# Query and key projections in seven block products instead of eight, on one core

## The chip, the cores and the metric

The kernel runs on one core of a Trainium2 chip. The metric is the device time of one execution in microseconds; less is better. Engines are named as in the profile: PE is TensorE (its matmuls; PEld its weight loads), DVE is VectorE, ACT is ScalarE, POOL is GpSimd, and SP is SyncE, which here only issues transfers. All numbers are fp32.

## The reference

The input is `x` of shape (8, 512, 32, 32): eight batch elements, 512 channels, 1024 positions. Two layers follow each other. Layer 0 is a group norm, a projection to queries, keys and values, attention in 8 heads of 64 channels, an output projection, a second group norm and a residual. Layer 1 is single-headed attention over 512 channels with normalized weights.

```python
# layer 0
hn = group_norm(x, gn1_scale, gn1_bias)
qkv = jnp.einsum('bchw,oc->bohw', hn, w_qkv) + b_qkv[None, :, None, None]
qkv = qkv.reshape(b * NHEAD, 3 * ch, n)
q, k, v = jnp.split(qkv, 3, axis=1)
scale = ch ** (-0.25)
wgt = jnp.einsum('bct,bcs->bts', q * scale, k * scale)
wgt = jax.nn.softmax(wgt, axis=-1)
a = jnp.einsum('bts,bcs->bct', wgt, v).reshape(b, c, h, w)
out = jnp.einsum('bchw,oc->bohw', a, w_proj) + b_proj[None, :, None, None]
out = group_norm(out, gn2_scale, gn2_bias)
return x + out
# layer 1: qkv = w_qkv x, divided by its rms; softmax(q k / sqrt(512)) v; w_out; (x + h) / sqrt(2)
```

The change concerns the lines that make `q` and `k` in layer 0.

## The kernel before

Every operation is issued through a wrapper that keeps the program's order on each engine, so the order in the text is the order in which each engine works. (All instructions carry the line of that wrapper, L34, in the profile; they are told apart by tile names.)

*Loops.* The outer loop runs over the eight elements `b`. For each, layer 0's attention runs in 32 steps `i`. The heads are taken in four pairs `j`, 8 steps to a pair; a step handles 128 query positions of both heads. Then come the end of layer 0 (`finish_layer0`), layer 1 (`Layer1.project`, which also holds the score stage with its four weight units, tiles `e`), and layer 1's products (tiles `po` with `e`), the last three of which are spread as fills over the next element's steps 0 to 2.

*A step* (`Heads.step`): the row maxima of both heads on DVE (`nm<-s`) and exponentials on ACT (`p<-s,nm`); then, on every second step from 5 on, the products with v of an earlier pair of steps (`po<-pT,v`); then the step's fill, usually one piece of a projection (`pqk`); then the scores of the next step (`s`); the transpose of the p of the step before on DVE (`pb<-p`), and four transfers on SP that rearrange it (`pT<-pb`); last, the reciprocal of the row sums on DVE and the scaling of p by it on POOL (`p<-p,tt`). What is in `later` follows the scaling; the adds of a projection (`due`) are there. On elements 1 to 6, POOL also normalizes a fourth of the next element's input in steps 1, 3, 5 and 7 (`hn<-hn,a,c`).

*Buffers.* Score tiles rotate through three PSUM buffers of two banks each, two tiles a step; so the second tile of step i+1 needs the buffer that the first exponential of step i frees. Projection pieces and value products rotate through two single banks. `pb` and the `p` tag have two buffers each.

*The projection of a pair* (`project_rows`), spread over the 8 steps of the pair before: for k, then q, and each half of the positions, one piece of 4 × 2 matmuls of 64 rows, which work side by side in the two halves of the array. The upper rows of channels give one PSUM bank, the lower rows the other; ACT evicts both (into `qk`, and into `v#`, the spare end of the `v` tile), and POOL adds them. That is 4 pieces, 8 block products (2 outputs, 2 halves of positions, 2 halves of rows), 32 matmuls a pair. A matmul of the program is two PE instructions in the profile. Pieces run in steps 0, 3, 4, 6 of pair 0's steps for elements from 1 on, and otherwise in steps 0, 2, 4, 6 of each pair's eight.

*Weights.* Three places in SBUF are shared in time: `qk` (the q and k weights, then layer 0's output operands, then layer 1's score operands), `v` (the v weights, then layer 1's value operands) and `p` (the Gram matrix of layer 1, which stays until the last element needs the plain output weights). `fetch` brings them back from DRAM copies through SP. `qk` and `v` are fetched in the score stage for the next element.

*Setup.* Weights are transposed on PE (`turn`), operands of seven-product schemes for the other projections are formed, and copies of all are stored to DRAM.

Of the kernel before, what the change touches and what calls it, by code (L numbers as in the profile page):

```python
# [8 lines left out]
F32 = mybir.dt.float32  # L9
I32 = mybir.dt.int32  # L10
AF = mybir.ActivationFunctionType
# [41 lines left out]
def attention_blocks_kernel(  # L53
# [52 lines left out]
    def big(name, lead=CI):  # L106

        return slots.take([P, lead, CI * N // lead], name)
# [14 lines left out]
    def run(pieces):  # L123
        for _ in pieces:
            pass
# [61 lines left out]
    cols = const.tile([P, NCOLS], F32, name="cols")  # L187
    bqs = const.tile([P, CI], F32, name="bqs")
    bpd = const.tile([P, 2], F32, name="bpd")

    def col(base, i):
        return cols[:, base + i : base + i + 1]
# [13 lines left out]
    def rsqrt(r, v, n, name):  # L206
# [3 lines left out]

    CH = C // 2
    places = {
        "qk": ("qk", [P, 2, CI, C]), "score": ("qk", [P, 7, 2, CH]),
        "v": ("v", [P, 7, 2, CH]), "value": ("v", [P, 7, 2, CH]),
        "proj": ("p", [P, CI, C]), "gram": ("p", [P, CI, C]), "proj7": ("qk", [P, 7, 2, CH]),
    }
    far = {
        name: dram.tile([P, CI, C] if name == "v" else shape, F32, tag=f"far_{name}", name=f"far_{name}")
        for name, (_, shape) in places.items()
    }  # L220
    near = {}
    far_rinv = dram.tile([NT, P], F32, tag="far_rinv", name="far_rinv")

    def place(name, b):
        tag, shape = places[name]
        near[name] = weights.tile(shape, F32, tag=f"w_{tag}", name=f"{name}_{b}")
        if name == "v":

            flat = near[name].rearrange("p k h c -> p (k h c)")
            near["v#"] = flat[:, CI * C :]  # L230
            near[name] = flat[:, : CI * C].rearrange("p (ci c) -> p ci c", ci=CI)
        return near[name]

    def fetch(name, b):
        SY.dma_start(out=place(name, b), in_=far[name])

    def turn(wrows, dst, k):

        for half in range(2):
            pt = ps_s.tile([P, 2, CI, P], F32, tag="sc", name=f"wT_{k}_{half}")  # L240
            for jj in range(2):
                for ci in range(CI):
                    PE.transpose(pt[:, jj, ci, :], wrows[:, 2 * half + jj, ci * P : (ci + 1) * P], ident)
            o = dst[:, :, 2 * half * P : 2 * (half + 1) * P].rearrange("p ci (jj o) -> p jj ci o", jj=2)
            for jj in range(2):
                if jj:
                    AC.copy(o[:, jj], pt[:, jj])
                else:
                    VE.tensor_copy(o[:, jj], pt[:, jj])


    def gn_stats(st, src, k):
# [85 lines left out]
    def project_qk(b, j, hn):  # L338

        qk = pair.tile([P, 2, N], F32, tag="qk", name=f"qk_{b}_{j}")  # L340
        kp = qk[:, 1, :].rearrange("p (be m) -> p be m", be=4)

        def pieces():
            for t in (1, 0):
                w = near["qk"][:, t]
                for th in range(2):
                    hs = slice(th * HN, (th + 1) * HN)
                    pm = bank(f"pqk_{b}_{j}_{t}_{th}")
                    run(matmuls(pm, [(w[:, ci, j * P : (j + 1) * P], hn[:, ci, hs]) for ci in range(CI)]))
                    if t == 0:  # L350
                        AC.activation(qk[:, 0, hs], pm, AF.Identity, bias=bqs[:, j : j + 1], scale=QSCALE0)
                    else:
                        AC.activation(
                            kp[:, :, th * P : (th + 1) * P],
                            pm.rearrange("p (m be) -> p be m", be=4),
                            AF.Identity,
                            bias=col(BK, j),
                        )
                    yield

        return qk, pieces()

    def project_rows(b, j, hn):

        qk = pair.tile([P, 2, N], F32, tag="qk", name=f"qk_{b}_{j}")
        kp = qk[:, 1, :].rearrange("p (be m) -> p be m", be=4)
        spare = near["v#"]

        def pieces():
            for t in (1, 0):
                w = near["qk"][:, t]
                scale = 1.0 if t else QSCALE0
                bias = col(BK, j) if t else bqs[:, j : j + 1]
                for th in range(2):
                    hs = slice(th * HN, (th + 1) * HN)
                    pms = [bank(f"pqk_{b}_{j}_{t}_{th}_{r}") for r in range(2)]
                    for ci in range(CI):
                        for r in range(2):  # L380
                            PE.matmul(
                                pms[r],
                                w[halves[r], ci, j * P : (j + 1) * P],
                                hn[halves[r], ci, hs],
                                start=(ci == 0),
                                stop=(ci == CI - 1),
                            )
                    to, rest = qk[:, 0, hs], spare[:, hs]
                    if t:

                        to = kp[:, :, th * P : (th + 1) * P]
                        rest = rest.rearrange("p (be m) -> p be m", be=4)
                        pms = [pm.rearrange("p (m be) -> p be m", be=4) for pm in pms]
                    AC.activation(to, pms[0], AF.Identity, bias=bias, scale=scale)
                    AC.activation(rest, pms[1], AF.Copy, scale=scale)
                    yield lambda to=to, rest=rest: PO.tensor_add(to, to, rest)

        return qk, pieces()

# [324 lines left out]
    class Layer1:  # L724
# [7 lines left out]
            self.right = self.rhs.columns  # L732
            self.e, self.sums = {}, {}

        def project(self):
            b, xt = self.b, self.xt
            v = self.v = big(f"v1_{b}", NT)
            xy = prob.tile([P, 2, N], F32, tag="p", name=f"xy_{b}")
# [1 line left out]
            for cj in range(CI):  # L740
# [5 lines left out]
                VE.tensor_mul(part if cj else acc, py.rearrange("p a f -> p (a f)"), xt[:, cj, :])  # L746
                if cj:
                    VE.tensor_add(acc, acc, part)
            if b + 1 == B - 1:
                fetch("proj", b + 1)  # L750

            ss = ps_m.tile([P, NT, 2], F32, tag="mm", name=f"ss_{b}")
            rinv = self.rinv = small.tile([P, NT], F32, tag="rinv", name=f"rinv_{b}")
# [105 lines left out]
                        square_sums()  # L859
                        broadcast()  # L860
            if b + 1 < B:
                fetch("qk", b + 1)
            sums = sum_u()
            for m in range(4):
                for k, _ in enumerate(value_unit(m).steps()):
                    if (m, k) in ((2, 0), (2, 4), (3, 1), (3, 5)):
                        next(sums, None)
            if b + 1 < B:
                fetch("v", b + 1)
            for m in range(4):  # L870
                run(weight_unit(m).steps())
            Seven.drain()
            Seven.half = None
            slots.give(f"u_{b}")
# [31 lines left out]
    gram = place("gram", 0)  # L906

    def turn_w0(t, name):
        near_t, far_t = (near["v"], far["v"]) if t == 2 else (near["qk"][:, t], far["qk"][:, t])
        turn(w0rows[t], near_t, name)  # L910
        SY.dma_start(out=far_t, in_=near_t)

    def operands(name, w, s7):

# [46 lines left out]
    SY.dma_start(out=far["gram"], in_=gram)  # L961
    VE.tensor_copy(cols[:, :GQKV], pcol)
    VE.tensor_scalar_mul(bqs, cols[:, BQ : BQ + CI], QSCALE0)
    VE.tensor_sub(bpd, cols[:, BP + 2 : BP + 4], cols[:, BP : BP + 2])
    next(coeffs)

# [24 lines left out]
    for name in ("w1_qk", "w1_vo"):  # L991
        slots.give(name)
    turn_w0(1, "k")
    v0_0 = big("v0_0", NT)
    v0 = project_v0(0, x0, v0_0)
    for _ in range(NT // 2):
        next(v0)
    turn_w0(0, "q")
    operands("value", value, [prob.tile([P, 4, 2, CH], F32, tag="p", name=f"value7_{i}") for i in range(2)])
    turn(wprow, proj, "p")  # L1000
    qk0, todo = project_qk(0, 0, x0)
# [2 lines left out]
    d3 = done3.rearrange("p (k h) c -> p k (h c)", k=2).rearrange("p k (i h c) -> p k i h c", h=2, c=CH)  # L1004
    operands("proj7", proj, [d3[:, k] for k in range(2)])
    SY.dma_start(out=far["proj"], in_=proj)
    for name in ("rows_kq", "rows_vp", "done1", "done2", "done3"):
        slots.give(name)


# [3 lines left out]
    heads.scores(0)  # L1014
    for b in range(B):
        hn, more = heads.hn, b + 1 < B
        todo = iter(())
        for i in range(STEPS):
            j, r = divmod(i, NB)
            due = []  # L1020

            projects = (i - LAG) % RG if not b or i not in (2, 3) else i == 3
            fill = [lambda: due.append(next(todo, None))] if projects else []
            early, later = [], []
            if i < CI:
                fill, later = fills[i] + fill, laters[i]
            if r == 0:
                if j + 1 < CI:
                    heads.qk[j + 1], todo = project_rows(b, j + 1, hn)
                elif more:  # L1030
                    qk_next, todo = project_rows(b + 1, 0, hn_next)
                if j + 1 == CI:
                    slots.give(f"hn_{b}")
                    if not more:
                        o_last = big(f"o_{b}")
                        todo = project_out_half(b, heads, o_last)
            later.append(lambda: [f() for f in due if f])

            if b and more and i % 2 and i < 2 * CI:
                later.append(lambda: norm1.apply(i // 2, PO))  # L1040
            if not b:
# [15 lines left out]
                if 0 <= k - 7 < CI // 2:  # L1057
                    for ci in range(2):
                        later.append(lambda ci=ci: norm1.apply(2 * (k - 7) + ci, PO))

            if i == STEPS - NB + 1:
                xt = big(f"x_{b}")
# [26 lines left out]
            finish_last(b, heads, xt, o_last, begun)  # L1089
        fetch("value", b)  # L1090
        one = Layer1(b, xt)
        one.project()
        hn_now, steps = hn_next, iter(())

        def norm_step():
# [75 lines left out]
```

## Time and profile before

| | us |
|---|---|
| median of 3 runs | 3283.85 (3283.36 to 3284.07) |
| the profiled execution | 3283.51 |
| its span, first to last instruction | 3281.5 |
| mean granted PE clock | 0.998 |
| one element, e.g. start of layer 1 (`py`) of element 1 to that of element 2 | 1136.99 − 739.74 = 397.25 |
| of it, the 32 attention steps (element 1, 494.22 to 679.92) | 185.7 |

The page gives busy time by engine; then the chain of work that ended last, as shares; then groups of instructions with their number, busy time, mean duration and the idle time before them. A row of the timeline has the start, the length, the engine, the operation with its tiles and shapes, how many instructions are merged, and in brackets the idle time before it with what ended it. Busy times of overlapping instructions are counted once, so a group's busy time is the time its engine gave to it.

### The profile page before, as it was taken

To read this page: it belongs to the slowest core of one execution; us is meant where nothing else is said; L and a number is where in the kernel's file an instruction comes from. 1 tells how busy PE (TensorE), PEld (TensorE's weight loads), DVE (VectorE), ACT (ScalarE), POOL (GpSimd) and SP (SyncE) were. 2 spreads that over 40 slices of the span, in tenths; PEclk is the share of its full clock that TensorE was granted. 3 is DMA by queue.
4 is the path that set the end of the run, shared out by engine and by line. 5 is a ranking of instruction groups with operands and counts; after the bars stand their busy time and mean duration, and the time that the engine had idled before them with its cause. 6 is when DMAs were issued, how large, how long until landed. Compare 5 with 4: busy or idle time off the path is not lost.

```text
span 3281.5 us, 35660 instructions
## 1 busy us (share of the span) xinstructions
PE 3251.9 (99%) x13178; PEld 1602.3 (49%) x13178; DVE 2124.0 (65%) x2869; ACT 1072.3 (33%) x1813; POOL 982.7 (30%) x857
## 2 busy tenths in 40 slices
PE   8999999999999999999999999999999999999899
PEld 4444544445444454444544445444454445444354
DVE  4696647855478555885458754686646866468653
ACT  2453114521145211551215512254123531145210
POOL 0352124511255012550215403253123521235121
PEclk9999999999999999999999999999999999999999
DMA  5675215751068411782127811377214762057500
GB/s 189 188 200 168 77 39 151 201 156 68 32 175 214 135 45 48 192 223 93 45 77 193 232 54 58 91 197 210 77 39 110 197 178 90 13 141 196 183 7 26
DMA packets 182707, 410.82 MB, mean 125 GB/s; under 512 B 27620, under 2 KB 27656, under 8 KB 176520
## 3 DMA queue, kind: packets, MB, share of 16 engines
q1 hardware_dynamic: 182416, 408.53, 44.0%
q8 instruction: 105, 1.72, 0.2%
q14 instruction: 66, 0.54, 0.0%
q10 hardware_dynamic: 120, 0.02, 0.0%
HBM read 112.48 MB, written 27.56 MB: 43 GB/s over the span
## 4 chain that ended last, share of the span: by engine, by line
PE 96%; DVE 1%; DMA 1%; SPq 1%; issue 1%; POOL 0%; ACTq 0%; DVEq 0%
PE po L34 27%; PE s L34 13%; PE pqk L34 13%; PE pv L34 7%; PE p_e_T L34 7%; PE p_e_B L34 5%; PE py L34 4%; PE p_u_T L34 3%; PE p_v_T L34 3%; PE p_o_T L34 3%; PE p_v_B L34 3%; PE p_u_B L34 3%; PE p_o_B L34 2%; DMA pT<-pb 1%; PE pG L34 1%; DVE pb L34 1%
## 5 line engine op out<-in xcount | busy, mean ns | idle before, releaser
L34 ACT ACTIVATE p<-s,nm 128x1024 f32<-128x1024 f32 x512 | 565.9, 1110 | 882.6 <-DVE nm L34 866.1
L34 POOL TENSOR_SCALAR p<-p,tt 128x1024 f32<-128x1024 f32 x512 | 565.9, 1118 | 942.4 <-DVE tt L34 942.4
L34 DVE TENSOR_REDUCE nm<-s 128x1 f32<-128x1024 f32 x512 | 603.2, 1220 | 206.7 <-PE s L34 206.5
L34 DVE STREAM_TRANSPOSE pb<-p 128x2048 f32<-128x2048 f32 x256 | 589.3, 2302 | 20.9 <-POOL p L34 18.7
L34 PE MATMUL s<-qk 64*128 64x512 f32 x2048 | 502.2, 602 | 0.0
L34 PE MATMUL po<-pT,v 128*64 128x256 f32 x4096 | 470.3, 382 | 3.7 <-DMA pT<-pb 3.6
L34 PE MATMUL pqk<-hn,qk 64*128 64x512 f32 (+1 forms) x2016 | 467.3, 590 | 0.0
L34 PE MATMUL po<-e,v 128*128 128x512 f32 x1024 | 451.7, 595 | 0.0
L34 PEld LDWEIGHTS po<-pT,v 128*64 128x64 f32 x4096 | 284.0, 137 | 227.1 <-ACT v L34 80.3
L34 PEld LDWEIGHTS pqk<-hn,qk 64*128 64x128 f32 (+1 forms) x2016 | 201.6, 187 | 245.0 <-issue 239.4
L34 PEld LDWEIGHTS po<-e,v 128*128 128x128 f32 x1024 | 191.9, 190 | 245.0 <-issue 236.4
L34 POOL TENSOR_TENSOR u<-u,xy 128x512 f32<-128x512 f32 x64 | 79.0, 1270 | 766.8 <-DMA xy<-far_rinv 471.9
L34 PEld LDWEIGHTS s<-qk 64*128 64x128 f32 x2048 | 190.8, 186 | 239.2 <-issue 236.7
L34 PE MATMUL pv<-v,hn 128*128 128x512 f32 x512 | 229.0, 598 | 0.0
L34 DVE TENSOR_TENSOR e<-e,p_e_T 128x512 f32<-128x512 f32 x160 | 107.1, 686 | 145.0 <-PE p_e_T L34 142.8
L34 ACT ACTIVATE e<-e,shift,rinv 128x512 f32<-128x512 f32 x128 | 100.9, 811 | 247.7 <-DVE e L34 247.7
L34 POOL TENSOR_TENSOR qk<-qk,v 128x512 f32<-128x512 f32 x124 | 158.3, 1276 | 46.8 <-ACT v L34 46.8
L34 POOL TENSOR_TENSOR esum<-esum,e 128x512 f32<-128x512 f32 x96 | 121.5, 1267 | 163.9 <-ACT e L34 161.4
L34 PEld LDWEIGHTS pv<-v,hn 128*128 128x128 f32 x512 | 94.6, 190 | 115.1 <-issue 114.8
L34 PE MATMUL p_e_T<-s,t 128*128 128x512 f32 x320 | 147.8, 592 | 0.0
L34 PE MATMUL py<-x,gram 128*128 128x512 f32 x320 | 141.3, 601 | 6.0 <-issue 6.0
L34 ACT COPY v<-pv 128x1024 f32<-128x1024 f32 x32 | 32.2, 1007 | 259.4 <-PE pv L34 246.8
(186 smaller groups left out, 3068.1 us busy)
## 6 DMA issues: line engine op xcount, KB each, us to landing
pT<-pb SPq DMA_DIRECT2D x1024, 256.0 KB, 4.2
hn<-in_x_dram SPq DMA_DIRECT2D x32, 512.0 KB, 5.2
x<-in_x_dram SPq DMA_DIRECT2D x32, 512.0 KB, 5.7
out_dram<-x SPq DMA_DIRECT2D x32, 512.0 KB, 2.6
score<-far_score SPq DMA_DIRECT2D x8, 1792.0 KB, 7.4
value<-far_value SPq DMA_DIRECT2D x8, 1792.0 KB, 7.3
qk<-far_qk SPq DMA_DIRECT2D x7, 2048.0 KB, 7.8
proj<-far_proj SPq DMA_DIRECT2D x7, 1792.0 KB, 10.4
```

The costliest lines, as they stand in the source:

```text
L34: return lambda *args, **kw: self._pin(call(*args, **kw))
```

## The change

For elements 1 to 7 and pairs 1 to 3, the projection is done as a product of 2 × 2 blocks: the rows of the left side are k and q, its columns (the sum's index) the upper and lower 64 rows of channels, and the right side has the two halves of positions as columns. Seven products of 4 matmuls each take the place of eight: pieces with 4, 8, 8 and 8 matmuls instead of 8, 8, 8, 8. Element 0, and pair 0 of each element, keep the old scheme.

- `operands_qk` forms the left operands once, on POOL, with two copies between partitions, and stores them (`far["qk7"]`, `far["qk0"]` for pair 0). q's weights are scaled when they are transposed, which therefore comes ahead of the first v projection.
- `Sums` forms the right operands for the next element inside weight units 1 to 3 of the score stage: 16 DVE operations on 64 partitions × 512, and three copies between partitions. They overwrite part of `hn` and use the front of the `v` tile (`t31`) and the `p` place (`t24`).
- `project_seven` makes a pair. POOL has eight adds for it. Those in the first list of `adds` run in the step of their piece, those in the second in the step after. `turned` reads a row with a step of four elements.
- The two places of `qk7` hold one pair each: pairs 1 and 2 are fetched in the score stage, pair 3 at step 8, pair 0 of the next element at step 16. `gram` (or `proj`) is fetched at step 21, `v` at step 24.

```diff
-    def turn(wrows, dst, k):
+    def turn(wrows, dst, k, scale=1.0):
...
+    class Sums:
+        def steps(self):
+            hn, t24, t31, (up, low) = self.hn, self.t24, self.t31, halves
+            t1, t2 = slice(0, HN), slice(HN, N)
+            SY.dma_start(out=t31[up], in_=hn[low, :, t2])
+            yield
+            for ci in range(CI):
+                VE.tensor_sub(t31[up, ci], t31[up, ci], hn[up, ci, t2])
+                yield
+            for ci in range(CI):
+                VE.tensor_add(t24[up, ci], t31[up, ci], hn[up, ci, t1])
+                yield
+            SY.dma_start(out=t24[low], in_=t24[up])
+            for ci in reversed(range(CI)):
+                VE.tensor_sub(hn[up, ci, t2], hn[up, ci, t2], hn[up, ci, t1])
+                if ci == 2:
+                    SY.dma_start(out=t31[low, :2], in_=hn[up, 2:, t2])
+                yield
+            for ci in range(CI):
+                VE.tensor_sub(t24[low, ci], hn[low, ci, t1], t24[low, ci])
+                yield
...
+    def project_seven(b, j, right):
...
+        adds = (
+            ([add(tmp[1], tmp[1], tmp[0])], []),
+            ([], []),
+            ([add(q2, q2, q1), add(k1, k1, turned(q2))], [add(q1, q1, tmp[0]), add(tmp[1], tmp[1], q2)]),
+            ([add(k1, k1, k2), add(k2, k2, turned(tmp[1]))], [add(q2, tmp[1], tmp[2])]),
+        )
+        def pieces():
+            for n, group in enumerate((3, 0, 1, 2)):
+                pms = [bank(f"pq7_{b}_{j}_{n}_{r}") for r in range(2)]
+                lo, hi = CI * group, min(CI * group + CI, 14)
+                for k in range(lo, hi):
+                    for r in range(2):
+                        PE.matmul(pms[r], w[halves[r], k, :], right(r, k), start=(k == lo), stop=(k == hi - 1))
...
+                AC.copy(*((tmp[0], pms[1]), (tmp[0], pms[1]), (k1, turned(pms[1])), (tmp[2], pms[1]))[n])
+                yield adds[n]
...
             if b + 1 < B:
-                fetch("qk", b + 1)
+                for j in (1, 2):
+                    fetch_qk(j, b + 1)
...
             if b + 1 < B:
-                fetch("v", b + 1)
+                place("v", b + 1)
+                self.next = Sums(b + 1, hn_next)
+                more = self.next.steps()
+                next(more)
             for m in range(4):
-                run(weight_unit(m).steps())
+                for _ in weight_unit(m).steps():
+                    if m:
+                        next(more, None)
...
+    def operands_qk():
+        (up, low), q, k = halves, near["qk"][:, 0], near["qk"][:, 1]
+        s = big("s_qk", 2 * CI)
+        s1, s2 = s[up, :CI, :], s[:, CI:, :]
+        s3 = block.tile([P, CI, C], F32, tag="pb", name="s3_qk")[up]
+        SY.dma_start(out=far["qk0"], in_=near["qk"][:, :, :, :P])
+        SY.dma_start(out=s1, in_=k[low])
+        PO.tensor_add(s1, k[up], s1)
+        PO.tensor_sub(s2[up], s1, q[up])
+        PO.tensor_sub(s3, q[up], k[up])
+        SY.dma_start(out=s2[low], in_=s2[up])
+        PO.tensor_sub(s2[low], q[low], s2[low])
+        for rows, lo, hi, src in (
+            (slice(0, P), 0, 4, q), (low, 4, 8, k[low]), (up, 4, 8, s2[up]), (up, 8, 12, s3), (up, 12, 14, s1[:, :2]),
+            (low, 12, 14, s1[:, 2:]), (low, 8, 12, s2[low]),
+        ):
+            SY.dma_start(out=far["qk7"][rows, lo:hi, :], in_=src[:, :, P:])
...
     turn_w0(1, "k")
+    turn_w0(0, "q")
+    slots.give("rows_kq")
+    operands_qk()
     v0_0 = big("v0_0", NT)
...
-    turn_w0(0, "q")
...
-                    heads.qk[j + 1], todo = project_rows(b, j + 1, hn)
+                    heads.qk[j + 1], todo = project_seven(b, j + 1, one.next.right) if b else project_rows(b, j + 1, hn)
...
+            if b and i == NB:
+                fetch_qk(CI - 1, b)
+            if b and i == 2 * NB and more:
+                fetch_qk(CI, b)
+            if b and i == STEPS - NB - 3:
+                fetch("gram" if more else "proj", b)
+            if b and i == STEPS - NB and more:
+                near["v"] = near["v_"].rearrange("p (ci c) -> p ci c", ci=CI)
+                SY.dma_start(out=near["v"], in_=far["v"])
```

## The prediction

> **What bounds the kernel now.** I read the busy shares first, then the chain of work that ended last, then one pair of steps in the timeline, then the waits.
>
> ```profile
> PE 3251.9 (99%) x13178; PEld 1602.3 (49%) x13178; DVE 2124.0 (65%) x2869; ACT 1072.3 (33%) x1813; POOL 982.7 (30%) x857
> PE 96%; DVE 1%; DMA 1%; SPq 1%; issue 1%; POOL 0%; ACTq 0%; DVEq 0%
> DVE nm L34 <- PE s L34: 206.5, 247, 9.0
> 600.00:610.67 10.67, 10.67 (x66) 5.22 (x64) 9.24 (x9) 6.14 (x13) 5.66 (x5) 1.00 0.79 199
> ```
>
> The last line is a stretch of time: its length, the busy us of PE, PE's weight loads, DVE, ACT and POOL, the granted clock, DMA's busy share and GB/s. TensorE (PE) sets the pace everywhere, at full granted clock (1.00). In the attention stage a pair of steps takes 10.67 us; VectorE (DVE) works 9.24 of it and waits for scores. DMA is 79% busy. So a saved PE microsecond counts only until another engine holds PE. How near that is, one pair shows (element 1; an even step e starts at 605.22):
>
> ```profile
> 605.22 1.99 PE L34 MATMUL s<-qk 64*128 64x512 f32 x8
> ...
> 607.04 3.60 PE L34 MATMUL pqk<-hn,qk 64*128 64x512 f32 x16
> 607.24 2.36 DVE L34 TENSOR_REDUCE nm<-s 128x1 f32<-128x1024 f32 x2 [0.90 <-PE s L34]
> 608.56 1.11 ACT L34 ACTIVATE p<-s,nm 128x1024 f32<-128x1024 f32 x1 [2.75 <-DVE nm L34]
> ...
> 610.48 1.88 PE L34 MATMUL s<-qk 64*128 64x512 f32 x8
> ...
> 611.96 2.21 POOL L34 TENSOR_SCALAR p<-p,tt 128x1024 f32<-128x1024 f32 x2 [3.31 <-DVE tt L34]
> ...
> 612.39 2.36 DVE L34 TENSOR_REDUCE nm<-s 128x1 f32<-128x1024 f32 x2 [0.53 <-PE s L34]
> ...
> 614.13 1.28 POOL L34 TENSOR_TENSOR qk<-qk,v 128x512 f32<-128x512 f32 x1
> ...
> 615.89 1.99 PE L34 MATMUL s<-qk 64*128 64x512 f32 x8
> ```
>
> PE does s(e), one projection piece (pqk), s(e+1), po, s(e+2) without a gap. Two things stand close behind it. The second half of s(e+1) needs the PSUM that the first exponential of step e frees: that ends at 609.67, 0.81 before 610.48. And POOL starts its projection add only after scaling p, at 614.13, 1.76 before s(e+2).
>
> **What is removed.** A pair's four pieces had 16 PE passes each; now they have 8, 16, 16, 16. Sixteen passes take 610.48 − 607.04 = 3.44, so 1.72 goes per projected pair: 21 pairs (three in each of seven elements), 36.1 us. The short piece runs in steps 0, 8 and 16.
> - Step 0: the fill also holds a layer-1 product of 7.1 us of PE, and the exponential is long done. The 1.72 counts in full.
> - Steps 8 and 16: the fill is the piece alone. s(e) → maximum → exponential still ends at 609.67; 0.1 later (the 0.12 between a maximum's end and its exponential is of that size) s(e+1) can go: 609.77 instead of 610.48. Gained 0.71; the other 1.01 turns into PE waiting for ScalarE. Bounds 0.55 to 0.81, by whether that handover costs 0.26 (all that PE lost in the wait of pA for DVE's ve) or nothing. DVE's next maximum can move 0.53 forward, and s(e+2) had 1.07 to spare over its exponential (614.82), so nothing later takes this back.
>
> Sum: 7 × (1.72 + 2 × 0.71) = 22.0 us.
>
> **What is added on POOL.** Four adds a pair become eight, and their order turns round. Before, K was finished two pieces ahead of its use. Now K's two last adds (k1 += k2, then k2 += turned sum) belong to the last piece, in steps 6, 14 and 22, and the first scores of the next pair, s(8), s(16), s(24), wait for the second one. It stands behind the scaling of p in the same queue: 614.13, plus two adds. The first is the old shape (1.28). The second reads one operand with a step of four elements, which no POOL row shows. Bounds: 1.28, if the step is free; 1.99, if it costs one more operand fetch, taken from these rows:
>
> ```profile
> L34 POOL TENSOR_SCALAR p<-p,tt 128x1024 f32<-128x1024 f32 x512 | 565.9, 1118 | 942.4 <-DVE tt L34 942.4
> L34 POOL TENSOR_TENSOR qk<-qk,v 128x512 f32<-128x512 f32 x124 | 158.3, 1276 | 46.8 <-ACT v L34 46.8
> ```
>
> One operand costs 1118/1024 = 1.09 ns an element, two 1276/512 = 2.49; the difference over 512 elements is 0.72. I take the middle, 1.64: the nearest row speaks for the low end, the growth with fetches for the high one. The adds end at 614.13 + 1.28 + 1.64 = 617.05; 0.1 on, s(e+2) starts at 617.15 instead of 615.89: 1.26 lost, with PE idle and nothing else to run (its queue is in order).
>
> At s(8) of elements 1 to 6 POOL is later still:
>
> ```profile
> 939.66 2.21 POOL L34 TENSOR_SCALAR p<-p,tt 128x1024 f32<-128x1024 f32 x2 [1.70 <-DVE tt L34]
> ...
> 941.86 1.19 POOL L34 TENSOR_SCALAR hn<-hn,a,c 128x1024 f32<-128x1024 f32 x1
> ```
>
> These are step 5's scaling and a normalization that rides on steps 1, 3, 5 and 7. Step 4's scaling ended at 936.71; its two adds now end at 939.63, just in time. Step 5 has two plain adds more (2.55) before the normalization, so POOL is free at 945.61, where step 6's scaling began at 945.17: 0.44 late, so s(8) loses 1.70. Sum: 6 × (1.70 + 2 × 1.26) + 3 × 1.26 = 29.1 us. With 1.28 the same working gives 0.89 and 1.33, 21.3 us; with 1.99 (step 4 overruns by 0.32) 1.61 and 2.37, 38.4 us.
>
> [...]
>
> **Sums of hn.** Sixteen DVE operations of 512 elements, 0.69 each by e<-e,p_e_T: 11.0 us an element, inside the last three weight units of the score stage.
>
> ```profile
> 805.00:855.00 50.00, 50.00 (x122) 22.99 (x121) 20.40 (x32) 14.54 (x20) 14.40 (x12) 1.00 0.06 22
> DVE e L34 <- PE p_e_T L34: 142.8, 64, 3.2
> ```
>
> DVE works 20.4 of 50 there and waits for PE up to 3.2 at a time: with 31.4 of 50 it still keeps up, and two pairs of products can queue in PSUM. Cost 0; without that cover 77 us in all. The first subtraction waits for a copy issued a whole unit (12 us) before, the t24 ones for one issued four products (6.9 us) before, against 4.2 to land; queued behind them are only e's sums.
>
> **Transfers.** Per element SP issues in attention steps, ahead of the pT copies of the same step: operands of pair 3 (0.92 MB, step 8), the next pair 0 (0.5 MB, 16), gram or proj (1 MB, 21), v (1 MB, 24). The score stage keeps pairs 1 and 2 in place of the whole qk, plus three copies of at most 0.5 MB, in a stretch with DMA at 6%. By qk<-far_qk (2 MB, 7.8 us) 0.92 MB takes 3.4, 1 MB 3.8. A pT copy has about 1.5 us before its pb buffer is wanted two steps on, DVE has 0.53 + 0.90 idle, and s(8), s(24) come 1.3 later anyway: 4.2 in all, so these just fit. But pair 3's rows are runs of 512 bytes, 112 for each of 16 engines; a 2 KB run of pT costs 0.79 × 10.67 / 64 = 0.13 us, so the upper bound is 14.7. Bounds for the kernel: 0 to 7 × 10.5 = 73 us; I take 2, by the 0.92 MB at qk's rate.
>
> **Setup.** The q transpose moves ahead of the first v projection (same work, no wait: the third PSUM buffer is free); POOL gets four operations of 2048 elements (5.1 each by the add row) ahead of value's copies, SP ten transfers ahead of value's stores. q is evicted by about 76.5 (k's four evictions ended at 73.67, 2.8 more for q's); with a copy of 4.2 POOL starts at 80.7 and has value's copies done at 103; the store lands 5.9 later at 109, and p of step 0 wants that buffer at 106.62. The exponential is 2.3 late, ending at 110.1; s(1), which needs it, starts at 112.30. Hidden by the v0 piece and the projection of step 0; 0 to 3 us, I take 0.
>
> **Sum.** −22.0 + 29.1 + 2 = +9.1 on the profiled execution's 3283.5 (2.0 outside its span), which is 0.3 below the median: 3293.
>
> **Rivals.**
> 1. *No change* (0.27): the strided add costs 1.28. −22.0 + 21.3 + 0 to 2: 3283 to 3285. For it: ScalarE reads s with the same step and shows no surcharge (1110 ns for 1024). Against: POOL's time does follow its fetches.
> 2. *Faster* (0.08): the scores are not held by POOL. Place: s(8), s(16), s(24). If both adds end before 615.89, 22.0 remain: 3262. It takes less than 1.66 us for the two, against 2.55 in the add row. The limit on the short piece stands even then, so 36 us are out of reach.
> 3. *Much slower* (0.14): short runs. If pair 3's fetch keeps the engines longer than about 4.2 us, DVE's transposes wait for pb, then the scores. At 7 us: 2.8 × 7 = 20 more, 3313. For it: DMA at 0.79. Against: the 4-byte packets of far_rinv<-rinv cost under 10 ns each (a share of 0.052 over 9 us, 1040 packets).
>
> **How the numbers follow.** My forecast has 0.51, with an own range of 3288 to 3303 (from an add of 1.4 to the 1.99 end). Less than 0.2% (6.6 us) can't be told from no change here. A fifth of my forecast and nearly all of rival 1 lie inside that: same 0.36. Slower: 0.41 + 0.14 = 0.55. Faster: 0.08 and a corner of rival 1, 0.09. The range, 3282 to 3309, leaves out rival 2 and about two thirds of rival 3.
>
> **What would show it.** Right: PE idle before s waiting for POOL, 21 times, 0.9 to 2.4 each; PE idle before s waiting for ACT, about 1.0, 14 times; PE busy down by some 36; POOL adds in two groups of shapes, the strided one above 1276. Wrong: s(16) starting without a wait; DVE pb waiting for pT; e's sums holding PE in the score stage.

## The result, and the profile after

| | before | after |
|---|---|---|
| median, us (lowest to highest) | 3283.61 (3282.42 to 3284.07) | 3303.87 (3300.65 to 3306.34) |
| ratio | | 1.0062, 95% interval 1.0044 to 1.0079 |
| span of the profiled execution | 3281.5 | 3303.5 |

The kernel became slower by about 20 us. The forecast was 3293, which is 9 us slower, with a range of 3282 to 3309: the direction is right, the size half of what came. The forecast's own range, 3288 to 3303, is missed by 0.9 us; the wider one holds because it takes in a third of rival 3, and not because the forecast had the term that made most of the loss.

The page of the changed kernel: the busy shares, the chain that ended last, and two groups (busy us, mean ns of one, then idle time before them and what ended it).

```profile
PE 3242.3 (98%) x13010; PEld 1597.1 (48%) x13010; DVE 2235.7 (68%) x2982; ACT 1064.0 (32%) x1813; POOL 1129.4 (34%) x945
...
PE 84%; POOL 5%; DMA 3%; DVE 3%; SPq 2%; ACT 1%; issue 1%; DVEq 0%; ACTq 0%; POOLq 0%
...
L34 DVE STREAM_TRANSPOSE pb<-p 128x2048 f32<-128x2048 f32 x256 | 590.0, 2305 | 79.1 <-DMA pT<-pb 53.3
L34 PE MATMUL s<-qk 64*128 64x512 f32 x2048 | 529.6, 604 | 26.0 <-POOL qk L34 25.1
```

PE lost 168 instructions, and the chain, 96% PE before, now has POOL, DMA and DVE in it. There are three new holds. The transposes of p waited 20.9 us in all before, 0.9 of it for `pT`; now 79.1, with 53.3 for `pT`. The waits of the changed kernel (us in total, times, longest) give the same by consumer:

```profile
PE s L34 <- POOL qk L34: 25.1, 21, 1.4
PEld s L34 <- ACT p L34: 20.0, 33, 1.0
PE po L34 <- DMA pT<-pb: 9.2, 7, 3.4
DVE pb L34 <- DMA pT<-pb: 53.3, 39, 3.5
```

The first is the wait for the key adds: 21 times, as forecast. The second has the wait of the short piece in it; it stood at 1.6 us, 7 times, before (and stands at 13.8, 21 times, in e1 below: 14 more, as many as forecast). PE shows it in the weight loads, as the timeline around s(8) of element 2 tells:

```profile
950.88 1.51 POOL L34 TENSOR_TENSOR qk<-qk,v 128x512 f32<-128x512 f32 x1
...
952.45 1.99 PE L34 MATMUL s<-qk 64*128 64x512 f32 x8 [1.42 <-POOL qk L34]
...
955.98 3.04 PE L34 MATMUL s<-qk 64*128 64x512 f32 x8
...
956.89 1.10 ACT L34 ACTIVATE p<-s,nm 128x1024 f32<-128x1024 f32 x1
957.04 0.30 PEld L34 LDWEIGHTS s<-qk 64*128 64x128 f32 x4 [0.87 <-ACT p L34]
```

POOL's strided add ends at 952.39 and s(8) follows at once, 1.42 late. Then s(9) starts early, at 955.98, and takes 3.04 in place of 1.88: its first half has a buffer, its second waits for the step's first exponential, which ends at 956.89 (where the second one starts). PE isn't idle meanwhile: in the single records behind this row, two matmuls run alone from 955.98 to 957.00, in one half of the array, where the same product before has them start in pairs. Such a stretch counts as busy. So PE's busy time fell by only 9.6 us (3251.9 to 3242.3), though 36 us of products are gone: the s group alone rose from 502.2 to 529.6.

The third hold, later in the same element:

```profile
1026.52 1.62 SPq L34 DMA_DIRECT2D gram<-far_gram  x1
...
1028.30 16.86 SPq L34 DMA_DIRECT2D pT<-pb  x12
...
1037.47 1.52 POOL L34 TENSOR_TENSOR qk<-qk,v 128x512 f32<-128x512 f32 x1
1039.04 1.99 PE L34 MATMUL s<-qk 64*128 64x512 f32 x8 [1.10 <-POOL qk L34]
1039.52 2.31 DVE L34 STREAM_TRANSPOSE pb<-p 128x2048 f32<-128x2048 f32 x1 [2.79 <-DMA pT<-pb]
```

SP issues gram's fetch (step 21), then the `pT` copies behind it; 13 us on, a transpose stands 2.79 us for a `pb` buffer that a late copy still reads. By the landing times in the trace, gram's fetch landed at 1036.72, 10.2 us after its issue began, and the first copy behind it at 1037.38, 9.1 after its own, where the median copy of this kernel takes 4.6. Three stretches of the changed kernel (length, busy us of PE, PEld, DVE, ACT, POOL, granted clock, DMA share, GB/s): behind gram's fetch, behind v's, and over the x loads:

```profile
1028.00:1038.67 10.67, 9.94 (x62) 4.73 (x58) 7.29 (x8) 6.12 (x11) 9.66 (x9) 1.00 0.94 294
1045.00:1055.67 10.67, 10.67 (x67) 5.37 (x65) 8.54 (x8) 6.58 (x14) 6.08 (x6) 1.00 0.96 301
1061.00:1083.00 22.00, 21.98 (x126) 10.56 (x126) 19.28 (x17) 12.75 (x23) 12.06 (x12) 1.00 0.93 265
```

DMA is busy 0.93 to 0.96 at up to 301 GB/s here, where an ordinary pair of steps had 0.79 at 199; the clock stayed at 1.00. But only the first two stretches are new. Over the x loads the kernel before was as busy, in steps 27 to 30 of the same element, and no step there was longer for it:

```profile
1050.41:1071.76 21.35, 21.35 (x131) 10.44 (x129) 18.32 (x17) 12.29 (x23) 11.33 (x10) 1.00 0.94 283
```

So the busy share alone doesn't show a hold.

**Where the time is.** I read the start of each step's first score product off PE's timeline. Element 3, from one step to the next, in us (the other elements from 1 to 6 are alike up to step 24):

| step | 0 | 7 | 8 | 9 | 15 | 16 | 17 | 23 | 27 | 29 |
|---|---|---|---|---|---|---|---|---|---|---|
| before | 12.52 | 5.42 | 5.26 | 5.41 | 5.42 | 5.25 | 5.42 | 5.41 | 5.42 | 5.42 |
| after | 10.80 | 6.90 | 3.54 | 6.58 | 6.60 | 3.54 | 6.57 | 6.59 | 6.52 | 6.26 |

Summed over the eight elements of the profiled executions, stage by stage (last column: from the last score product to layer 1's first product), each kernel less the one before:

| | steps 0–7 | 8–15 | 16–23 | 24–30 | end of layer 0 |
|---|---|---|---|---|---|
| after | −1.9 | +4.3 | +4.3 | +8.1 | +7.6 |
| e1, gram late | −2.0 | +4.3 | +4.3 | +0.4 | +2.3 |
| e2, x late | −2.0 | +4.3 | +4.6 | +9.8 | +0.5 |
| e3, both late | −0.4 | +5.8 | +4.3 | 0.0 | +1.3 |
| e4, no fetch at steps 8 and 16 | −1.9 | +4.3 | +4.2 | +7.8 | +10.6 |
| e5, short piece doubled | +10.1 | +8.3 | +8.3 | 0.0 | +3.0 |
| e6, no step in the last add | −2.9 | +2.8 | +2.5 | 0.0 | +1.9 |
| e7, one add on DVE | −8.3 | +0.2 | −1.5 | +2.3 | +3.1 |
| e8, normalizations later | −10.6 | −1.4 | −2.5 | +1.9 | +2.2 |
| e9, gram from ScalarE's queue | −2.0 | +4.6 | +13.5 | +1.7 | +1.8 |
| e10, gram in quarters | −2.0 | +5.5 | +4.8 | +2.9 | +5.4 |
| e11, spread transfers | −10.6 | +1.6 | −2.5 | +0.3 | +0.7 |

Layer 1 up to the next element's first scores is the same in each of them within 0.1 us (1062.3 over seven elements), and the setup within 1.0. So products and adds cost −1.9 + 4.3 + 4.3 = 6.7 us, close to the 7.1 that the prediction's −22.0 + 29.1 makes; and 15.7 us lie in steps 24 to 30 and the end of layer 0, for which it had 2. Some 2.2 of them stand at the end of element 7, which has no gram to fetch; there the runs range from 0 to 2.6 with the same code, and why stays open. Each row is one execution, and not always a middling one: that of e9 is its fastest (3302.69), that of e10 is 2.9 above its median.

### The profile page after: what moved, and what is told of

Same layout as the page of the kernel before. It is cut to its first block, busy times and chain, and to the rows that moved or that the text cites. A ratio compares the mean times of both kernels' runs of the same rounds, so it can differ in the third digit from the quotient of the medians.

```text
span 3303.5 us, 35734 instructions
## 1 busy us (share of the span) xinstructions
PE 3242.3 (98%) x13010; PEld 1597.1 (48%) x13010; DVE 2235.7 (68%) x2982; ACT 1064.0 (32%) x1813; POOL 1129.4 (34%) x945
## 4 chain that ended last, share of the span: by engine, by line
PE 84%; POOL 5%; DMA 3%; DVE 3%; SPq 2%; ACT 1%; issue 1%; DVEq 0%; ACTq 0%; POOLq 0%
PE po L34 22%; PE s L34 11%; PE p_e_T L34 7%; PE pv L34 7%; PE p_e_B L34 5%; PE pq L34 4%; PE py L34 4%; PE pqk L34 3%; PE p_u_T L34 3%; PE p_v_T L34 3%; DMA pT<-pb 3%; PE p_o_T L34 3%; PE p_v_B L34 3%; PE p_u_B L34 2%; POOL p L34 2%; PE p_o_B L34 2%
## 5 line engine op out<-in xcount | busy, mean ns | idle before, releaser
L34 POOL TENSOR_SCALAR p<-p,tt 128x1024 f32<-128x1024 f32 x512 | 565.9, 1118 | 851.8 <-DVE tt L34 833.2
L34 DVE STREAM_TRANSPOSE pb<-p 128x2048 f32<-128x2048 f32 x256 | 590.0, 2305 | 79.1 <-DMA pT<-pb 53.3
L34 PE MATMUL s<-qk 64*128 64x512 f32 x2048 | 529.6, 604 | 26.0 <-POOL qk L34 25.1
L34 PEld LDWEIGHTS s<-qk 64*128 64x128 f32 x2048 | 199.9, 186 | 282.0 <-issue 223.5
L34 PE MATMUL pq<-hn,qk 64*128 64x512 f32 x588 | 191.2, 590 | 0.0
L34 POOL TENSOR_TENSOR esum<-esum,e 128x512 f32<-128x512 f32 x96 | 132.9, 1386 | 151.6 <-ACT e L34 149.0
L34 PE MATMUL pqk<-hn,qk 64*128 64x512 f32 (+1 forms) x672 | 163.3, 590 | 0.0
L34 PE MATMUL p_e_B<-u,x 128*128 128x512 f32 x256 | 116.4, 592 | 0.0
```

The source lines that it names most:

```text
L34: return lambda *args, **kw: self._pin(call(*args, **kw))
```

## The experiments

In all of them the theory is that of the prediction: 21 short pieces gain, 21 waits for POOL lose, and the remainder is bulk transfers that hold up the `pT` copies. The rivals are that the remainder comes from POOL's longer queue (e1 to e3) or from pair 3's short runs (e4), and that the short piece counts in full everywhere (e5).

**e1: gram's fetch after the attention.**

```diff
-                fetch("gram" if more else "proj", b)
+                if not more:
+                    fetch("proj", b)
...
             fetch("proj7", b)
+            if b:
+                fetch("gram", b)
```

> Gram's fetch (1 MB) moves from step 21 to the end of layer 0, where DMA is little used. Theory (the loss of steps 24 to 31 and of the end of layer 0, 15 us in all over elements 1 to 7, comes from gram's, v's and x's transfers that together hold up the pT copies): about half of it goes, 3293 to 3299, and the first transpose of step 23, which waits 2.8 us for pT in element 2, waits no more. Rival (the loss comes from POOL's longer queue, which delays the p buffers): no change, 3302 to 3306.

Measured: 3291.62 (3290.00 to 3294.17), ratio 1.0023 [1.0014, 1.0033]. That is 12.3 us below the changed kernel, more than expected. Waits, then the same stretch of time as above (e1 is 2.4 us further on in its steps by then):

```profile
DVE pb L34 <- DMA pT<-pb: 13.6, 17, 1.9
```

```profile
1028.00:1038.67 10.67, 9.56 (x62) 4.73 (x60) 8.06 (x9) 6.12 (x11) 9.66 (x9) 1.00 0.81 197
```

DMA is back at 0.81 and 197 GB/s, the transposes wait 13.6 us for `pT` in place of 53.3, and steps 24 to 30 take what they took before (+0.4). One fetch in each of six elements was nearly the whole of the unforeseen loss, and POOL's queue, which e1 leaves as it is, was not its cause.

**e2: the x loads of elements 1 to 6 after the last step; e3: both edits.**

```diff
-            if 0 <= i - (STEPS - NB + 1) < CI:
+            if not (b and more) and 0 <= i - (STEPS - NB + 1) < CI:
...
+            if b:
+                for c in range(CI):
+                    load_x(b, xt, c)
             ta = big(f"ta_{b}").rearrange(
```

> x's four loads (0.5 MB each) of elements 1 to 6 move from steps 25 to 28 to after the last step. Theory (transfers hold up pT): the waits in steps 26 to 31 go, those of steps 23 to 25, behind gram and v, stay; 3292 to 3298. Rival (POOL's queue): no change, 3302 to 3306.

> Both moves together. Theory (transfers): steps 24 to 31 return to 37.3 us and the end of layer 0 to 65.1 in every element, 3289 to 3291, and runs scatter less. If v's fetch at step 24 alone is enough to hold pT up, 2 to 5 us more. Rival (POOL's queue): 3302 to 3306.

Measured: e2 3300.38 (3299.71 to 3303.04), 1.0051 [1.0036, 1.0065]; e3 3291.94 (3290.22 to 3294.76), 1.0024 [1.0015, 1.0033]. e2 is a miss: only 3.5 us. The end of layer 0 is as it was (+0.5), but steps 24 to 30 still lose 9.8. The traces show how the delay is carried on, and it is not as a backlog of bytes: in step 24 of element 2 (1039.04 to 1044.30) DMA falls to 0.42 busy. It goes with the order on SP. The copies of the late transpose are issued late, and v's fetch of step 24 behind them: 5.1 to 6.2 us after s(24) starts in the changed kernel and 4.3 to 6.6 in e2, against 3.0 to 3.4 in e1. The next copies then follow 1.4 to 2.3 us after v's fetch (3.3 to 3.6 in e1), and the transpose that waits for them is held 0.4 to 4.1 us, against 0 to 1.9. No run moved v's fetch alone. With gram out of the way, moving x gives nothing that can be told from e1. In e3's profile 3 us of delay came up in steps 0 to 15 of one element, where e3 changes nothing.

**e4: no fetch for pair 3 and none for the next pair 0.** Those two are projected with the operands that happen to be there; the work is the same, the values are not.

```diff
-        if j < CI:
+        if j == CI - 1:
+            pass
+        elif j < CI:
             SY.dma_start(out=near["qk7"][:, (j - 1) % 2], ...)
         else:
             ...
-            SY.dma_start(out=to, in_=far["qk0"])
```

> Leaves out the fetches of steps 8 and 16, so pair 3 and the next element's pair 0 are projected with other pairs' operands. Theory (only the transfers from step 21 on cost): no change within 2 us, 3301 to 3306, steps 8 to 24 stay at 43.3 us per pair. Rival (pair 3's short runs hold up pT, as the prediction feared): 5 us or more faster.

Measured: 3306.62 (3303.87 to 3310.84), 1.0069 [1.0054, 1.0084], just above the expected band; the transposes still waited 49.4 us for `pT`. No gain: the fetches at steps 8 (in 512-byte runs) and 16 (in rows of 4 KB) cost nothing in the changed kernel. Rival 3 had the right mechanism in the wrong place.

**e5: on e1, the short piece issues each of its matmuls twice**, so that it is as long as the others (its product comes out doubled).

```diff
-                for k in range(lo, hi):
+                ks = [*range(lo, hi)] * (2 if n == 0 else 1)
+                for m_, k in enumerate(ks):
...
```

> On e1's kernel, the short piece issues its four matmuls twice, so it has 16 passes as a piece of the old scheme (its product comes out doubled). Theory (in steps 8 and 16 the first exponential holds the next scores, so the short piece is worth 0.57 there and 1.72 only in step 0): 7 x (1.72 + 2 x 0.57) = 20.0 us slower than e1, 3311 to 3313; steps 8 and 9 together take 10.67 again. Rival (a piece's PE time counts in full everywhere): 36 us slower, 3327 to 3329.

Measured: 3311.58 (3310.30 to 3313.05), 1.0084 [1.0068, 1.0099], so 20.0 above e1. The steps of element 3: step 0 back from 10.80 to 12.52, steps 8 and 9 from 10.10 to 10.67. That is 7 × (1.72 + 2 × 0.57) = 20.0, and the wait of the weight loads for the exponential is back at 1.6 us, 7 times. The 36 us of removed products were worth 20.

**e6: on e1, the add `k2 += turned sum` reads without a step** (the columns of k are then in another order).

```diff
-add(k2, k2, turned(tmp[1]))
+add(k2, k2, tmp[1].rearrange("p (be m) -> p be m", be=4))
```

> On e1's kernel, the last add of a pair (k2) reads its second operand without the step of four elements, so k's columns come out in another order. Theory (the step costs 0.25 us and the scores wait for it): the waits of s(8), s(16), s(24) shrink by 0.25 each, 21 x 0.25 = 5.2 us faster than e1, 3285 to 3288. Rival (the step costs nothing and 1.52 us is something else): no change, 3290 to 3294.

Measured: 3287.31 (3283.85 to 3291.69), 1.0011 [1.0002, 1.0020]: 4.3 below e1. The timeline at s(16) of element 2:

```profile
990.37 1.28 POOL L34 TENSOR_TENSOR qk<-qk 128x512 f32<-128x512 f32 x1
991.73 1.27 POOL L34 TENSOR_TENSOR qk<-qk,v 128x512 f32<-128x512 f32 x1
...
993.05 1.99 PE L34 MATMUL s<-qk 64*128 64x512 f32 x8 [0.85 <-POOL qk L34]
```

The add takes 1.27 in place of 1.52, and PE waits 0.85 in place of 1.10. The step costs 0.25 us, a fifth; the other 0.85 is the order of the adds, as rival 1 had it.

**e7: on e1, `k1 += k2` on VectorE; e8: also the normalizations of steps 5 and 7 in steps 9 and 11.**

```diff
-([add(k1, k1, k2), add(k2, k2, turned(tmp[1]))]
+([lambda: VE.tensor_add(k1, k1, k2), add(k2, k2, turned(tmp[1]))]
```

```diff
-            if b and more and i % 2 and i < 2 * CI:
-                later.append(lambda: norm1.apply(i // 2, PO))
+            if b and more and i in (1, 3, 9, 11):
+                later.append(lambda: norm1.apply((1, 3, 9, 11).index(i), PO))
```

> On e1's kernel, the add before it (k1 += k2) moves from POOL to DVE, behind the reciprocal of the same step. Theory (POOL's second add alone makes the scores late): the waits of s(16) and s(24) go, s(8) keeps about 0.3; 6 x (1.1 + 2 x 1.1) + 3 x 1.1 = 23 us faster than e1, 3268 to 3272. Rival (DVE has no room: 0.53 idle against an add of 0.69, its next maximum and transpose come late): 5 us faster at most, or slower.

> e7, and POOL's normalizations of the next input move from steps 5 and 7 to steps 9 and 11. Theory (POOL is late in step 6 because of the normalization in step 5): s(8) waits no more, 2 us faster than e7, 3266 to 3270. Rival (s(8) waits for something else): as e7.

Measured: e7 3278.49 (3276.96 to 3281.91), 0.9986 [0.9977, 0.9995]; e8 3274.67 (3272.04 to 3279.36), 0.9973 [0.9963, 0.9984]. Both are a little faster than the kernel before (0.14% and 0.27%). e7 gains less than expected, 13.1 against 23; e8 gains 3.8 on e7 against 2, and lies above its band because e7 does. The timeline of e7 at s(16) of element 2 shows one reason:

```profile
983.54 0.67 DVE L34 TENSOR_TENSOR qk<-qk 128x512 f32<-128x512 f32 x1
983.72 2.57 POOL L34 TENSOR_SCALAR p<-p,tt 128x1024 f32<-128x1024 f32 x2 [0.84 <-DVE tt L34]
...
986.25 1.54 POOL L34 TENSOR_TENSOR qk<-qk,v 128x512 f32<-128x512 f32 x1
...
987.85 0.30 PEld L34 LDWEIGHTS s<-qk 64*128 64x128 f32 x4 [0.59 <-POOL qk L34]
```

While DVE adds, POOL's scaling takes 2.57 in place of 2.21. So it is each time: of the two scalings of such a step, the one that starts inside DVE's add takes 1.47 to 1.55 in place of 1.12, in all 21 of e7 (and 1.47 to 1.53 in all 21 of e8 and of e11), though it overlaps the add by only 0.49 to 0.57. Over the kernel the scaling group grew from 565.9 us to 573.9, so 0.38 for each of the 21 adds, and 0.2 of wait is left at s(16) and s(24) (step 15 at 5.61 against 5.42) and 0.58 at s(8), where step 5's normalization still stands in the queue; e8 takes that to 0.20. By the stage sums the first 24 steps gained 16.2 of e1's losses in e7. The other part of the miss is that transfer delays came up again: +2.3 and +3.1 in the last two stages, and 0.6 to 1.3 in steps 8 to 15 of three elements; the transposes wait 37.2 us for `pT` (13.6 in e1).

**e9: on the changed kernel, gram's fetch from ScalarE's queue; e10: in four quarters, steps 21 to 24.**

```diff
-                fetch("gram" if more else "proj", b)
+                if more:
+                    AC.dma_start(out=place("gram", b), in_=far["gram"])
+                else:
+                    fetch("proj", b)
```

```diff
-                fetch("gram" if more else "proj", b)
+                if more:
+                    place("gram", b)
+                else:
+                    fetch("proj", b)
+            if b and more and 0 <= i - (STEPS - NB - 3) < CI:
+                k = i - (STEPS - NB - 3)
+                SY.dma_start(out=near["gram"][:, k], in_=far["gram"][:, k])
```

> The change with one edit: gram's fetch at step 21 is issued on ScalarE's queue instead of SP's. Two readings of the 12 us that this fetch costs. (a) Its bytes: 1 MB stands in the DMA engines ahead of the pT copies; then the issuing queue matters little: 3299 to 3306, and DVE still waits about 50 us in sum for pT. (b) SP's queue: the one long issue (1.6 us) and the order behind it hold the pT copies; then the time falls to that of the late fetch, 3290 to 3294, and DVE waits under 20 us for pT. ScalarE's own cost of the issue: at most 1.6 us x 6 elements, with the exponential some 0.8 ahead of its use, so up to 5 us on top in (b).

> The change with one edit: gram's fetch of 1 MB at step 21 becomes four of 256 KB, one in each of steps 21 to 24, the same bytes on the same queue. If a delay arises only where one burst is longer than the slack of the pT copies (1.5 to 2 us), quarters of about 1 us fit, and the time falls to that of the late fetch: 3290 to 3295. If it is the sum of bytes in these steps that is too much (DMA busy 0.8 before), nothing is won: 3300 to 3306. Between them: 3295 to 3300.

Measured: e9 3306.51 (3302.69 to 3308.75), 1.0068 [1.0054, 1.0082]; e10 3297.93 (3292.84 to 3301.69), 1.0039 [1.0023, 1.0054]. In e9 SP's long issue is gone (0.36 us on ScalarE's queue in place of 1.62) and the cost is not: 3306.51 against 3303.87, so the bytes are enough, from either of these two queues. But the rows put only 14.4 us of the transposes' waits down to `pT`, where about 50 were expected, and the loss sits in steps 16 to 23 (+13.5 where e1 has +4.3). The timeline of e9, element 2:

```profile
1022.74 0.36 ACTq L34 DMA_DIRECT2D gram<-far_gram  x1
...
1033.73 2.31 DVE L34 STREAM_TRANSPOSE pb<-p 128x2048 f32<-128x2048 f32 x1 [1.50 <-POOL v L34]
...
1041.29 1.13 PE L34 MATMUL s<-qk 64*128 64x512 f32 x4 [2.69 <-POOL qk L34]
```

ScalarE issues the fetch about 4 us earlier than SP did (0.3 after s(21) starts, against 4.7), so one transpose earlier is late, by 1.50; the maximum, the scaling of p and POOL's two adds follow it, and s(24) waits 2.69 in place of 1.10. The row puts the 1.50 down to an add that the transpose doesn't read; but the trace's semaphore times (the moments at which the parts of a transfer report that they have landed) show the copy: of the four copies that this transpose waits for, the last was issued at 1026.83 and its last part landed at 1033.55, 0.18 before the transpose starts. In each of elements 1 to 6 one such wait behind a late copy stands there, 0.7 to 3.6 us, 9.6 in sum, against the 9.2 that these steps lose beyond e1. Steps 24 to 30 lose little in e9, and v's fetch is issued 2.6 to 3.1 us after s(24), as in e1.

e10 wins back 5.9 us, about half; its four runs spread over 8.9, so this is rough. The waits behind the first quarters are all but gone (by the semaphore times 1.9 us at the transposes that waited 16.3 in the changed kernel); those behind step 24 are not (10.9 of 16.4). There the last quarter and the whole of v's fetch stand in one step, so e10 doesn't tell one long burst from the sum of bytes. In all the transposes wait 31.9 us for `pT`.

**e11: e8, with v's fetch in quarters in steps 24 to 27 and x late.**

```diff
-                SY.dma_start(out=near["v"], in_=far["v"])
+            if b and more and 0 <= i - (STEPS - NB) < CI:
+                k = i - (STEPS - NB)
+                SY.dma_start(out=near["v"][:, k], in_=far["v"][:, k])
```

> The version with gram's fetch late, k1 += k2 on VectorE and the normalizations moved, with two further edits: v's fetch of 1 MB at step 24 becomes four of 256 KB in steps 24 to 27, and the x loads of elements 1 to 6 move behind the last step. By the steps of the profiled run of that version (3272.0), the transfers of steps 24 to 31 and the start of layer 0's end still cost 1.2 + 0.6 + 1.0 + 0.5 + 0.7 = 4 us, and the steps before it 0.9; its median is 2.6 higher, by what I take for the same delays in other places. If both edits take these away: 3268 to 3271, with a narrower spread. If the split only moves the delays: 3272 to 3276.

Measured: 3271.71 (3269.80 to 3274.84), 0.9964 [0.9951, 0.9976]: the best here, 11.8 us below the kernel before, 3.0 below e8 and just above the hoped range. Waits of e11:

```profile
DVE pb L34 <- DMA pT<-pb: 19.3, 17, 2.4
PE s L34 <- POOL qk L34: 1.5, 3, 0.7
```

Steps 24 to 30 and the end are down to +0.3 and +0.7. What is left moved: steps 8 to 15 take 4.1 us more than steps 16 to 23, with pair 3's fetch the one bulk transfer issued in them. By the semaphore times 13.6 us of the transposes' waits for `pT` in e11 stand at the copies issued right behind that fetch, where e1 has 1.5 and the changed kernel 2.5. In e4's surroundings it cost nothing; here the scores no longer come late at s(8), which would hide it. e11 without this fetch was not tried.

## Why the prediction was right, and where it was off

**What the removed products are worth: right.** Predicted 1.72 in step 0 and 0.71 in steps 8 and 16, 22.0 us; measured 1.72 and 0.57, 20.0 (e5). The hand-over from the exponential's end to the second half of s(e+1) costs 0.15 to the weight load (956.89 to 957.04) and some 0.1 more (the first two matmuls behind it take 0.69 in place of 0.59), not 0.1 in all: near the bound of 0.55. It was to be seen as PE idle waiting for ScalarE, 14 times, with PE busy down by 36: the 14 waits came, but in the weight loads, and busy time hides them because half the product goes on.

**What POOL's order costs: right.** Predicted 1.26, and 1.70 at s(8) of six elements, 29.1 us; measured 1.18 and 1.49. By the steps above that is 6 × 1.49 + 15 × 1.18 = 26.6, which with −20.0 gives the 6.7 of the stage sums. That 6.7 lies so near the predicted 7.1 is in part luck: the gain was put 2.0 too high, the loss 2.5 too high. The middle of 1.28 and 1.99 for the strided add, 1.64, stands against 1.52: the step of 16 bytes in one of its two operands added 0.25 us, 20% (1.52 against 1.27 in e6), so the middle was nearer than either bound.

**Transfers: the mis-sized term.** "I take 2", against 15.7. The mechanism (a fetch longer than the slack makes DVE wait for `pb`, then the scores) was there, as rival 3, priced on pair 3's 512-byte runs at step 8. It happened with gram's unbroken rows at step 21, which e1 shows to be worth 12.3 of it. The step that failed is "these just fit": it set 3.8 us (3.9 by the row's own sizes) against 4.2 of slack, with the 3.8 taken from a fetch in the score stage, where DMA was at 6%; in steps already at 0.79 the same bytes share the engines with 1 MB of `pT` copies a step, and gram's fetch took 10.2 us to land, the copy behind it 9.1. It also priced each fetch by itself, though gram's delay pushes v's fetch against the next copies (e2). It added up three slacks, of which the late s(24) is spent before the late transpose comes (1039.04 and 1039.52). The same paragraph's other bound, up to 10.5 us an element, did hold the truth: 15.7 / 7 = 2.2. And "DVE pb waiting for pT" stood among the prediction's own signs of being wrong; it came, and here is where the prediction was wrong.

**Sums of hn at 0: right.** Layer 1 up to the next scores is the same to 0.1 us over seven elements. **Setup at 0:** s(0) of element 0 came 0.18 later.

**The rivals.** No change would have needed the strided add to be free: e6 makes it so, and with gram's fetch moved is at 3287, against 3283 to 3285 there. The row that spoke for it, 1110 ns, is no read with the step, for the exponential takes s in order; in the kernel before it is k's eviction that ScalarE reads so, in 686 ns against 685 for q's. Faster: the place was right, and e7 and e8 show the price, since with POOL's hold out of the way the change does win; the limit on the short piece holds there too.

## What to carry to other kernels

Don't price a bulk fetch by the rate of a quiet stage: among copies that kept DMA 0.79 busy, 1 MB took 10.2 us to land (element 2) in place of the 3.8 expected. What it costs is read from the slack of the copies issued behind it, not from the busy share: here 0.5 MB a step (x, before) and 0.92 MB where the next scores came late anyway (step 8) went in for nothing, 1 MB at step 21 did not. Moving that fetch to a later stage won 12 us, splitting it about 6. When work is taken from the bounding engine, ask step by step what it runs into next (here an exponential's buffer, and the last add in another engine's queue), and look at what stands in one queue ahead of the next product (moving one of the two last adds to another engine won 13 us). Nor can PE's busy time be read as a saving: here it counted the stretches in which half of a product waited, and fell by 9.6 us where 36 us of products went.

## What the runs showed that was not expected

- Where one of the moved adds on DVE overlapped work on POOL in e7, the one that started second took longer. The scaling that starts inside the add takes 1.47 in place of 1.12 us, and the add its 0.67. At s(8) of elements 1 to 6 it is DVE's add that starts inside a normalization on POOL: it takes 1.05 to 1.06, the normalization its usual 1.19. In e8, with those normalizations moved, no add takes longer than 0.72. In the changed kernel POOL's sums of e (`esum<-esum,e`) went from 1267 to 1386 ns, in the stage that got the sums of hn; it cost nothing there.
- The length of a fetch's runs did not tell its cost: 0.92 MB in 512-byte runs at step 8 cost nothing (e4), 1 MB in unbroken rows of 8 KB at step 21 cost 12 us over six elements (e1). No run put one in the other's place.
- The four runs of the changed kernel spread over 5.7 us, the four of before over 1.7 (23 later ones over 4.1). That the transfers do it isn't shown: with gram's fetch moved ten runs spread over 4.2 in e1, over 7.8 in e6.
